# Moving the attention preparation ahead of the threshold search and merging the list's comparisons, in a deformable-convolution and attention kernel

## The chip, the cores and the metric

The kernel runs on one core of a Trainium2 chip. The metric is the device time of one execution in microseconds. Before the change the median of three runs is 10539.41 us (10536.02 to 10541.7). One further execution was profiled; its times are a little longer than those of the bare runs, and every time that is read from a trace belongs to it.

Names: PE is TensorE, DVE is VectorE, ACT is ScalarE, POOL is GpSimd, and SP is the engine from which most DMAs are issued. Line numbers (L1300) are those of the kernel before. In the kernel after, lines from L553 on stand four lower down the file, and those behind the new `yield` five lower.

## The reference

The input x holds four images of 64 x 64 positions (4096 tokens) with 256 channels, in fp32. The first layer is a deformable convolution: from the group-normalised image it computes, for each token, group and tap, an offset and a mask, samples the image bilinearly at the moved places, and projects the sum. The second layer treats each image as a sequence of 4096 tokens. Additive attention comes first and a feed-forward network (FFN) on a selection of the tokens second. Cut to what matters here:

```python
x = x + conv(group_norm(x))                       # bilinear samples at learned offsets
t = tokens(x)
n = layer_norm(t)
beta  = tanh((n @ Wt)[:, :, None] + (n @ Wx)[:, None, :] + bh)   # 4096 x 4096 x 32
a     = softmax(beta @ Wa)
t = t + a @ n
n = layer_norm(t)
w = n @ wr + br                                   # one weight per token
sel = the 2047 tokens with the largest w
y = gelu(n[sel] @ w1 + b1) @ w2 + b2              # 256 -> 1024 -> 256
n[sel] = y * w[sel] where selected, else 0;   t = t + that
```

## The kernel before, in words

**Stages in time.** First the offsets and sampling weights of all four images are computed (until about 815 us). Then image 0 is sampled alone (about 815 to 1480 us). Then, for each image n, there is a stretch *between the loops* (L1408 to L1430) and the attention loop of image n (`attention`, from L860). The FFN of image 3 ends the kernel. The sampling of image n+1 runs beside both the stretch and the attention loop of image n.

**The stretch between the loops.** It has three generators, and each `yield` in them ends one portion of instructions:

- *main*, written m: `feed_forward(n-1)`. It loads all tokens of the attention's result into one large tile `v2` (eight DMAs on SP) and the weights w1, w2, b1, b2 (L1247 to L1251). It computes 32 dot products with wr ("dots", four portions of eight). It searches the 2047th largest weight four bits at a time (`kth_largest`, L1200): in each round DVE counts for 15 candidates how many weights are not below them, PE adds the counts over the partitions (pcn, L1207), and DVE picks the digit. `positions` turns flags into places by a matmul and a running sum. Then POOL writes every token to its place in a DRAM array by 32 indirect DMAs, the *scatter* (L1300). ACT computes the base output rows for all tokens and stores them (L1312). At last the selected tokens are worked through in four chunks of 512. The load of a chunk (L1332, on SP) waits for all 32 scatters. ACT normalises (L1340); PE transposes and DVE copies (xT); POOL adds (L1346); PE multiplies by w1 (ph, L1360), ACT applies gelu, PE multiplies by w2 (py, L1366), DVE scales and adds (L1369), and POOL scatters the rows to the output (L1373).
- *prep*, written o: `attention_prep(n)`. It loads the image's tokens t into `v` (L770, eight DMAs), takes mean and variance of 32 tiles (eight portions of four), and normalises on ACT (L802, 32 activations, one portion). Then come eight *units* of 512 tokens with three portions each: transposes (ptt, L780) and a copy vT, projections (pq, L812), a cut at zero on DVE (mm), selections by matmul (pk, L827, and pf, L833), exponentials on ACT (kf, L828, and qe, L835), a store of qe to DRAM, and a minimum over pk on DVE (least).
- *sampling*, written s: `sample_image(n+1)`. Its first portion is `list_tokens` (L537): tokens whose offsets are too large for the main path are listed by comparing, for each of 32 tiles, a row of slot numbers with the token's slot on DVE (`oh`, L552) and multiplying on PE into `pl` (L553). All further portions are *steps*; there are 440 in an image (`STEPS`). Most are one product of 128 x 1024 on DVE (L697) or one addition (L705). A product needs a weight tile `wb` by an SP DMA (L688, two buffers here). Some steps project the sum (pmo, L721, with its POOL addition) or belong to the far tokens (their gathers, L626, run only beside attention).

A string `turns` deals out the portions: each letter asks its generator for one more. What is left of main and prep is emitted after the string, and what is left of the sampling is dealt out beside the attention loop, one step in every block (256 blocks of 512 queries by 128 keys), and a second step in as many blocks as are needed to bring it to its end.

**Who fixes the order.** The DVE instructions of main and prep go through `pinned` (L259, which therefore is the line of them all), and the products and sums of sampling and all of attention's through `keep`: these stay in program order on their engine. A tile scheduler places the others, DMAs among them, and the buffers of the pools bound how far ahead anything may run. Engines and their DMA queues work in order.

For n = 0 there is no `feed_forward`, and for n = 3 there is nothing to sample, so that the letter s does nothing. The stretches that hold all the change are those of n = 1, 2 and 3; the string of n = 0 and the last FFN, which runs alone, keep their order.

Of the kernel before, what the change touches and what calls it, by code (L numbers as in the profile page):

```python
# [9 lines left out]
F32 = mybir.dt.float32  # L10
I32 = mybir.dt.int32
AF = mybir.ActivationFunctionType
ALU = mybir.AluOpType
# [3 lines left out]
P = 128  # L17
NB, H, W, C = 4, 64, 64, 256
L = H * W
NT = L // P  # L20
# [25 lines left out]
def layers_kernel(ctx: ExitStack, tc: tile.TileContext, a, out: bass.AP):  # L46
    nc = tc.nc
# [19 lines left out]
    def load_const(pool, name, shape, src):  # L67
        t = pool.tile(shape, F32, name=name)
        nc.sync.dma_start(out=t, in_=src)  # L69
        return t  # L70
# [139 lines left out]
    tok = cb.tile([P, NT, 2], F32, name="tok")  # L210
    slotr = cb.tile([P, P], F32, name="slotr")
# [22 lines left out]
    S = SimpleNamespace(bank=True, wants=False, gather=True, left=0, tables=[])  # L234

    def bank_taken():
        S.wants = not S.bank
        return S.wants

    @contextmanager  # L240
    def scope(*pools):

        with ExitStack() as st:
            for name, bufs, psum in pools:
                kw = {"space": PSUM} if psum else {}
                setattr(S, name, st.enter_context(tc.tile_pool(name=name, bufs=bufs, **kw)))
            yield
            for name, _, _ in pools:
                delattr(S, name)
# [267 lines left out]
    def positions(fl, vec):  # L517

        pp = S.ps_m.tile([P, 2, NT], F32, tag="pm", name="pp")
        nc.tensor.matmul(pp[:, 0, :], below, fl, start=True, stop=True)  # L520
        nc.tensor.matmul(pp[:, 1, :], ones, fl, start=True, stop=True)
        before = [S.two.tile([P, NT], F32, tag=f"bf{i}", name=f"bf{i}") for i in range(2)]
        vec.tensor_copy(before[0], pp[:, 1, :])
        for i in range(5):
            w = 1 << i
            vec.tensor_copy(before[1][:, :w], before[0][:, :w])
            vec.tensor_add(before[1][:, w:], before[0][:, w:], before[0][:, : NT - w])
            before.reverse()
        sl = before[1]
        vec.tensor_sub(sl, before[0], pp[:, 1, :])  # L530
        vec.tensor_add(sl, sl, pp[:, 0, :])
        return sl, before[0][:, NT - 1 :]

    def list_tokens(n):

        while bank_taken():
            yield  # L540
        fl = S.two.tile([P, NT], F32, tag="fl", name="fl")
        nc.vector.tensor_scalar(fl, omax[:, n, :], 1.0, None, ALU.is_gt)
        sl, total = positions(fl, nc.vector)
        nc.vector.tensor_copy(large[:, n : n + 1], total)

        nc.vector.tensor_scalar(sl, sl, 1.0, None, ALU.add)
        nc.vector.tensor_mul(sl, sl, fl)
        nc.vector.tensor_scalar(sl, sl, -1.0, None, ALU.add)
        pl = S.ps_m.tile([P, 2], F32, tag="pm", name="pl")
        for i in range(NT):  # L550
            oh = S.sb.tile([P, P], F32, tag="oh", name="oh")
            nc.vector.tensor_scalar(oh, slotr, sl[:, i : i + 1], None, ALU.is_equal)  # L552
            nc.tensor.matmul(pl, oh, tok[:, i, :], start=(i == 0), stop=(i == NT - 1))  # L553
        ls = S.two.tile([P, 2], F32, tag="ls", name="ls")
        nc.vector.tensor_copy(ls, pl)

        uf = S.smp.tile([P, 1], F32, tag="uf", name="uf")
        nc.vector.tensor_mul(uf, ls[:, 1:2], spare)
        nc.vector.tensor_sub(uf, spare, uf)
        nc.vector.tensor_add(uf, uf, ls[:, 0:1])  # L560
        return uf
# [106 lines left out]
    def sample_image(n, depth=1):  # L668
# [3 lines left out]

        S.left = STEPS
        uf = yield from list_tokens(n)
        yield
        exact = []
# [63 lines left out]
    def sample_any(n):  # L740

        num = nc.values_load(large[0:1, n : n + 1], min_val=0, max_val=L)
        with tc.If(num > P), scope(
            ("smp", 2, 0), ("two", 2, 0), ("sb", 2, 0), ("dn", 1, 0), ("ps_t", 1, 1), ("ps_m", 1, 1)
        ):
            cur = S.two.tile([P, 1], F32, tag="cur", name="cur")
            nc.vector.tensor_copy(cur, part)
            with tc.For_i(0, NT, 1):
                exact = []
                for _ in exact_rows(n, cur, exact):  # L750
                    pass
                put_rows(n, *exact[0])
                nc.vector.tensor_scalar(cur, cur, float(P), None, ALU.add)
# [14 lines left out]
    def load_tokens(v, src):  # L768
        for s in range(8):
            nc.sync.dma_start(  # L770
                out=v[:, 4 * s : 4 * s + 4, :C],
                in_=src[s * 512 : (s + 1) * 512].rearrange("(t p) c -> p t c", p=P),
            )
# [470 lines left out]
    def feed_forward(n, vec):  # L1244


        v = S.one.tile([P, NT, C + 4], F32, tag="big", name="v2")  # L1247
        load_tokens(v, t2_d[n])
        w1 = load_const(S.one, "w1", [P, CC, FF], a["L1_ffn_w1"].rearrange("(k p) f -> p k f", p=P))
        w2 = load_const(S.one, "w2", [P, FF // P, C], a["L1_ffn_w2"].rearrange("(k p) f -> p k f", p=P))  # L1250
        b1 = load_columns(S.one, "b1", a["L1_ffn_b1"])  # L1251
# [33 lines left out]
        sl, _ = positions(eq, vec)  # L1285
# [3 lines left out]
        sl, _ = positions(gt, vec)  # L1289
# [65 lines left out]
        for s in range(NSORT // 512):  # L1355
# [7 lines left out]
            for t in range(4):  # L1363
# [8 lines left out]
                m = min(P, NSEL - s * 512 - t * P)  # L1372
# [30 lines left out]
    for n in range(NB):  # L1403
        with scope(("att", 1, 0), ("smp", 2, 0), ("dn", 1, 0)):
            v = S.att.tile([P, NT, C + 1], F32, name="v")
            kf = S.att.tile([P, 2, L], F32, name="kf")

            sampling = sample_image(n + 1) if n + 1 < NB else iter(())  # L1408
            S.gather = False
            with scope(  # L1410
                ("one", 1, 0), ("two", 2, 0), ("sb", 2, 0), ("row", 2, 0), ("rp", 3, 0),
                ("ps_d", 2, 1), ("ps_n", 1, 1), ("ps_m", 3, 1),
            ):


                main = feed_forward(n - 1, pinned) if n else iter(())
                prep = attention_prep(n, v, kf, pinned)
                if n:
                    turns = (
                        "mo" + "m" * 5 + "mo" * 6 + "m" + "ooo" + "s" + "oss" * 2 + "m" + "oss" * 7 + "m" + "oss" * 3  # L1420
                        + ("m" + "ossss" * 3 + "msss" * 4) * 4
                    )
                else:
                    turns = "o" * 10 + "s" + "os" * 24
                for turn in turns:
                    next({"m": main, "o": prep, "s": sampling}[turn], None)
                for rest in (main, prep):
                    for _ in rest:
                        pass
            S.gather = True  # L1430
            with scope(
                ("two", 2, 0), ("sb", 2, 0), ("rp", 6, 0), ("qp", 2, 0),
                ("ep", 2 * PVB + 1, 0), ("ap", 1, 0), ("ps_d", 2, 1), ("ps_n", 3, 1), ("ps_m", 1, 1),
            ):
                attention(n, v, kf, [sampling])
        attention_any(n)
        if n + 1 < NB:
            sample_any(n + 1)
    with scope(("one", 1, 0), ("two", 2, 0), ("sb", 3, 0), ("row", 2, 0), ("ps_d", 2, 1), ("ps_m", 4, 1)):
        for _ in feed_forward(NB - 1, nc.vector):  # L1440
            pass
# [36 lines left out]
```

## Time and profile before

| What | us |
|---|---|
| median of three runs | 10539.41 (10536.02 to 10541.7) |
| profiled execution | 10563.61 |
| its span, first to last instruction | 10561.9 |
| attention loops, first D (L894) to last row sum, n = 0, 1, 2, 3 | 1997, 1912, 1912, 1798 |
| stretch from there to the next first D, before n = 1, 2, 3 | 372, 370, 294 |
| scatter of n = 1 (L1300), first to last | 3680.4 to 3720.7 |
| first ph of n = 1 (L1360) | 3784.5 |
| last FFN alone: end of the scatter, first ph, end of the last py | 10420.8, 10432.8, 10546.3 |

How to read the views. The page counts how long each engine was busy and how many instructions it ran. A *windows* row gives one stretch of time: its borders and length, then for each engine the busy time and in brackets the number of instructions that started, then the mean TensorE clock that was granted (1.00 is full speed), the mean share of the DMA engines in use and GB/s. A *timeline* row gives the start, the time taken, the engine, the line, the operation, output and inputs, the shape, how many alike were joined into the row, and in square brackets how long the engine had been idle before and what ended that ("remote" and "issue" name no instruction). SPq is the DMA queue of SP: its rows last as long as the queue was held. A *group* row gives the busy time and mean duration in nanoseconds of all instructions alike.

### The profile page before, as it was taken

What the parts mean: (1) busy time and instruction counts of PE and PEld (TensorE: products, weight loads), DVE (VectorE), ACT (ScalarE), POOL (GpSimd) and SP (SyncE); (2) the same over time, 40 slices, a digit from 0 to 9 for tenths busy, and PEclk for the clock granted to TensorE, in tenths of its full rate; (3) what the DMA queues carried; (4) which work ended last, traced back from release to release, by engine and by line L of the source; (5) the groups of instructions that cost most, each with busy time, mean ns of one, the idle gap of its engine ahead of it and who ended that gap; (6) DMA issues with size and microseconds to landing.
All of it is one profiled execution on the core that took longest, in us unless ns stands there. A gap on an engine that the chain in (4) does not pass through costs nothing. (4 is left out here: it accounts for less than half of the span.)

```text
span 10561.9 us, 115936 instructions
## 1 busy us (share of the span) xinstructions
PE 9008.4 (85%) x38460; PEld 4375.8 (41%) x38460; DVE 8547.2 (81%) x13406; ACT 7377.6 (70%) x8389; POOL 5265.2 (50%) x3059
## 2 busy tenths in 40 slices
PE   7882029999999678999999589999999699999995
PEld 4551014444444343444444344444444344444443
DVE  7776879898989778989899679899898357777772
ACT  4450018888888528888888438888888379999991
POOL 0004307676555326767655327676555155555552
PEclk8985569999999889999999789999999799999997
DMA  3336752222222252212111352222111300000002
GB/s 119 107 138 180 206 167 70 61 67 64 70 64 73 98 167 60 52 55 58 51 55 50 116 152 53 53 54 54 52 59 41 101 13 9 10 8 7 7 5 75
DMA packets 381330, 766.00 MB, mean 73 GB/s; under 512 B 49105, under 2 KB 212593, under 8 KB 380689
## 3 DMA queue, kind: packets, MB, share of 16 engines
q1 hardware_dynamic: 324432, 678.78, 20.3%
q0 software_dynamic: 30144, 45.87, 2.9%
q10 hardware_dynamic: 26112, 33.56, 0.9%
q8 instruction: 309, 5.06, 0.2%
q14 instruction: 333, 2.72, 0.1%
HBM read 580.88 MB, written 177.14 MB: 72 GB/s over the span
## 5 line engine op out<-in xcount | busy, mean ns | idle before, releaser
L909 DVE TENSOR_TENSOR r<-nn,r 128x512 f32<-128x512 f32 x6144 | 3943.0, 683 | 861.5 <-PE nn L904 805.9
L904 PE MATMUL nn<-qn,kf 32*128 32x512 f32 (+1 forms) x12288 | 4518.8, 640 | 132.7 <-DVE r L909 95.8
L994 POOL TENSOR_TENSOR r<-r 128x1024 f32<-128x1024 f32 x1024 | 2708.8, 2645 | 2645.4 <-DVE r L909 2625.3
L988 ACT ACTIVATE r<-d 128x1024 f32<-128x1024 f32 x3072 | 3117.2, 1015 | 1085.4 <-DVE r L998 699.9
L894 PE MATMUL d<-qf,kf 32*128 32x512 f32 (+1 forms) x12288 | 3338.1, 632 | 76.5 <-DMA qf<-qf 43.1
L990 ACT ACTIVATE r<-r 128x1024 f32<-128x1024 f32 x3072 | 3124.1, 1051 | 32.6
L904 PEld LDWEIGHTS nn<-qn,kf 32*128 32x128 f32 (+1 forms) x12288 | 1399.4, 185 | 1902.1 <-DVE r L909 1450.5
L932 PE MATMUL pv<-v,et 128*128 128x257 f32 x8192 | 2105.3, 400 | 15.0 <-DVE acv L956 15.0
L932 PEld LDWEIGHTS pv<-v,et 128*128 128x128 f32 x8192 | 1507.6, 194 | 975.5 <-issue 768.6
L894 PEld LDWEIGHTS d<-qf,kf 32*128 32x128 f32 (+1 forms) x12288 | 1018.0, 186 | 1340.3 <-issue 736.1
L996 POOL TENSOR_TENSOR r<-r 128x512 f32<-128x512 f32 x1024 | 1335.8, 1304 | 92.7 <-DVE r L909 17.1
L705 DVE TENSOR_TENSOR ac<-ac,prd 128x1024 f32<-128x1024 f32 x768 | 991.8, 1291 | 8.8
L697 DVE TENSOR_TENSOR prd<-xs,wb 128x1024 f32<-128x1024 f32 x768 | 977.7, 1273 | 15.2 <-DMA wb<-wt 12.0
L626 POOL DMA_INDIRECT ga<-tab,tii x576 | 718.3, 1247 | 207.3 <-issue 117.7
L916 ACT ACTIVATE et<-et,nshift 128x512 f32<-128x512 f32 x1024 | 723.8, 707 | 28.2 <-DVE et L1001 28.2
L998 DVE TENSOR_TENSOR r<-r 128x512 f32<-128x512 f32 x1024 | 723.6, 707 | 4.1 <-POOL r L994 3.7
L1001 DVE TENSOR_TENSOR et<-r 128x512 f32<-128x512 f32 x1024 | 698.1, 682 | 0.4
L115 ACT ACT_TABLE_LOAD x9 | 11.5, 1283 | 799.3 <-DVE mv L259 703.0
L721 PE MATMUL pmo<-outwp,ac 128*128 128x256 f32 x512 | 135.7, 416 | 469.1 <-DVE ac L705 431.2
L480 POOL MEMSET w<- 128x1600 f32 x16 | 22.9, 1432 | 675.0 <-PE ptw L497 352.3
L721 PEld LDWEIGHTS pmo<-outwp,ac 128*128 128x128 f32 x512 | 100.8, 205 | 521.4 <-DVE ac L705 304.5
L420 PE MATMUL pc<-xn,diag 128*128 128x512 f32 x576 | 262.2, 609 | 33.4 <-ACT xn L366 33.4
(344 smaller groups left out, 5282.7 us busy)
## 6 DMA issues: line engine op xcount, KB each, us to landing
wb<-wt SPq DMA_DIRECT2D x800, 512.0 KB
tab<-tb SPq DMA_DIRECT2D x128, 256.0 KB
v<-t SPq DMA_DIRECT2D x64, 512.0 KB
xs<-xp SPq DMA_DIRECT2D x32, 680.0 KB
xp<-xp SPq DMA_DIRECT2D x32, 544.0 KB
xt<-in_x_dram SPq DMA_DIRECT2D x32, 512.0 KB
xr<-in_x_dram SPq DMA_DIRECT2D x64, 256.0 KB
t<-xr SPq DMA_DIRECT2D x64, 256.0 KB
```

Source lines behind the costliest of these rows:

```text
L697: keep(nc.vector.tensor_tensor(pr.rearrange("p (r w) -> p r w", w=W), src, wb.rearrange("p (r w) -> p r w", w=W), ALU.mult,))
L705: keep(nc.vector.tensor_add(ac[:, f, :], ac[:, f, :], pr))
L894: keep(nc.tensor.matmul(d[:, j, :], kf[g, blk, rows(kt)], qs[q][0][g, blk, :], start=True, stop=True))
L904: keep(nc.tensor.matmul(nn, kf[g, blk, rows(kt)], qs[q][1][g, blk, :], start=True, stop=True))
L909: keep(nc.vector.tensor_tensor(r[:, j, :], ns[j], r[:, j, :], ALU.mult))
L916: keep(nc.scalar.activation(ets[b], ets[b], AF.Exp, bias=nshift))
L932: keep(nc.tensor.matmul(pv, ets[b0 + i][:, rows(j)], v[:, k0 + i, :], start=(i == 0), stop=(i == PVB - 1)))
L988: keep(nc.scalar.activation(rs[b, p], ds.pop((b, p)), AF.Ln))
L990: keep(nc.scalar.activation(rs[b, p], rs[b, p], AF.Exp, scale=-1.0))
L994: keep(nc.gpsimd.tensor_tensor(rs[b, 1], rs[b, 1], rs[b, 2], ALU.add))
L996: keep(nc.gpsimd.tensor_tensor(rs[b, 1][:, 0], rs[b, 1][:, 0], rs[b, 3][:, 0], ALU.add))
L998: keep(nc.vector.tensor_add(rs[b, 1][:, 1], rs[b, 1][:, 1], rs[b, 3][:, 1]))
```

## The change

It has three parts.

1. In `list_tokens` the slots of two tiles are compared by one `tensor_tensor` on 128 x 2 x 128 elements with both inputs broadcast, in place of two `tensor_scalar` on 128 x 128. The 32 matmuls stay as they are.
2. A `yield` behind the load of v2 splits the first portion of main in two.
3. The string `turns` for n of 1 and more is another.

```diff
         for i in range(NT):
-            oh = S.sb.tile([P, P], F32, tag="oh", name="oh")
-            nc.vector.tensor_scalar(oh, slotr, sl[:, i : i + 1], None, ALU.is_equal)
-            nc.tensor.matmul(pl, oh, tok[:, i, :], start=(i == 0), stop=(i == NT - 1))
+            if i % 2 == 0:
+                oh = S.sb.tile([P, 2, P], F32, tag="oh", name="oh")
+                nc.vector.tensor_tensor(
+                    oh, slotr.rearrange("p (o q) -> p o q", o=1).to_broadcast([P, 2, P]),
+                    sl[:, i : i + 2].rearrange("p (t o) -> p t o", o=1).to_broadcast([P, 2, P]), ALU.is_equal,
+                )
+            nc.tensor.matmul(pl, oh[:, i % 2], tok[:, i, :], start=(i == 0), stop=(i == NT - 1))
...
         load_tokens(v, t2_d[n])
+        yield
         w1 = load_const(S.one, "w1", [P, CC, FF], a["L1_ffn_w1"].rearrange("(k p) f -> p k f", p=P))
...
                     turns = (
-                        "mo" + "m" * 5 + "mo" * 6 + "m" + "ooo" + "s" + "oss" * 2 + "m" + "oss" * 7 + "m" + "oss" * 3
-                        + ("m" + "ossss" * 3 + "msss" * 4) * 4
+                        "om" + "o" * 9 + "s" + "om" * 12 + "m" + "oss" * 4 + "m" + "oss" * 8 + "m"
+                        + ("m" + "s" * 8 + "msss" * 4) * 4
                     )
```

Read letter by letter, the strings deal out this:

| | before | after |
|---|---|---|
| first loads | v2 with w1, w2, b1, b2, then v | v, then v2 |
| w1, w2, b1, b2 | with v2 | with the first dots |
| statistics of v (8 portions) | 6 beside the search, 2 behind the scatter's letter | all ahead of the dots |
| normalising | behind the scatter's letter | ahead of the dots |
| the list | behind the scatter's letter | ahead of the dots |
| portions of units beside dots and search | none | 12 of 24 |
| from the scatter's letter to that of the first chunk | 9 portions of units, 18 steps | 12 portions, 24 steps |
| from there to the first ph | 3 portions, 6 steps | none |
| in the FFN's four chunks | 12 portions, 96 steps | 80 steps |
| steps left for the attention loop | 320 | 336 |

## The prediction

> **What bounds the kernel now.** I read the page first, then the busy time by stretches, then the timelines of single engines inside the stretches that the change touches. The page:
>
> ```profile
> span 10561.9 us, 115936 instructions
> PE 9008.4 (85%) x38460; PEld 4375.8 (41%) x38460; DVE 8547.2 (81%) x13406; ACT 7377.6 (70%) x8389; POOL 5265.2 (50%) x3059
> ```
>
> No engine is full over the whole; the stages have different limits, and the change touches only the stretch between two attention loops. By the first D (L894) and the last row sum of each image these stretches are 3607 to 3979 (372 us), 5910 to 6280 (370) and 8211 to 8505 (294). Stretches by engine (stretch, length, then busy us and instructions of each engine, granted clock of PE, DMA share, GB/s):
>
> ```profile
> 3607.00:3680.00 73.00, 8.79 (x32) 7.65 (x32) 52.06 (x261) 19.09 (x34) 0.15 (x1) 0.51 0.71 237
> 3680.00:3735.00 55.00, 22.45 (x83) 18.41 (x84) 14.94 (x65) 17.44 (x34) 31.83 (x33) 0.50 0.22 78
> 3735.00:3785.00 50.00, 42.04 (x83) 15.91 (x83) 46.59 (x59) 11.57 (x16) 3.24 (x1) 0.69 0.58 172
> 3785.00:3850.00 65.00, 62.35 (x199) 35.84 (x198) 47.43 (x46) 26.48 (x32) 7.32 (x5) 0.97 0.52 167
> 3850.00:3955.00 105.00, 89.01 (x311) 58.23 (x309) 91.49 (x89) 25.93 (x31) 24.84 (x16) 0.95 0.62 199
> 3955.00:3980.00 25.00, 1.79 (x10) 0.63 (x10) 9.20 (x13) 0.00 (x0) 6.76 (x4) 0.54 0.46 134
> 3980.00:5910.00 1930.00, 1869.22 (x8293) 862.16 (x8286) 1733.09 (x2611) 1645.89 (x1792) 1232.12 (x685) 0.98 0.19 52
> ```
>
> Search and scatter (first two rows): PE idle at half clock; during the scatter (3680 to 3721) DVE is idle for 40 of 55 us. Then DVE and PE together bound the FFN, with sampling and the second half of the preparation on DVE. In all DVE is busy 261.7 of 373 us, idle 111. In attention DVE is busy 90%.
>
> Why is the scatter empty? The timelines of POOL, DVE, ACT and SP (start, us, operation, count, and in brackets the idle time before it with its releaser):
>
> ```profile
> 3683.02 0.96 POOL L1300 DMA_INDIRECT sort<-v,rif  x1 [0.30 <-issue]
> ```
>
> ```profile
> 3707.23 0.29 DVE L552 TENSOR_SCALAR oh<-slotr,bf 128x128 f32<-128x128 f32 x1 [5.34 <-remote]
> 3731.59 1.22 DVE L259 COPY vT<-ptt 128x1024 f32<-128x1024 f32 x1
> ```
>
> ```profile
> 3687.04 15.84 ACT L802 ACTIVATE v<-v,lnm,lnr 128x256 f32<-128x256 f32 x32 [1.79 <-DMA sort<-v,rif]
> 3702.90 1.28 ACT L828 ACT_TABLE_LOAD   x1
> ```
>
> ```profile
> 3649.04 92.32 SPq L688 DMA_DIRECT2D wb<-wt  x4
> 3741.67 0.92 SPq L1332 DMA_DIRECT2D big<-sort  x2
> ```
>
> The 32 scatters take 1.27 us each (40.3 us). Beside them stand only the list's comparisons, which crawl on late PE results, and the normalising. The first unit of the preparation starts at 3731. The sorted rows' load stands on SP behind the wb loads, 21 us past the last scatter (3720.7).
>
> **The change part by part.** For n=1:
>
> (1) *Everything of the preparation up to the normalising, and the list, come ahead of the search.* Today the first count (pcn, L1207) is at 3632.4 and the threshold at 3670.1: 37.7 us, of which 5 x 4 row statistics (2.12 us per four in the timeline) are 10.6, so the bare search is 27.1. Afterwards DVE starts at about 3617.7, when the first tokens land, as now. Eight groups of statistics (17 us) interleave with the list: 16.1 us where it runs alone (819.7 to 835.6), mostly waiting for its 32 matmuls, with under 10 us of DVE. Together some 28 us, to 3646. The 32 activations (15.84) and the table load (1.28) come next; the first exponential is behind them on ACT, the reduction least is pinned on DVE behind that, and the dots are pinned behind least. So this wait, hidden in the scatter today, is bare: +17.1, to about 3667 with PE's part. Dots (13.5) and the next unit's copies: first count near 3682, 50 us later than now.
>
> (2) *Four units of the preparation beside the search.* A unit is 8 transposes, 4 pq, 4 pk and pf: at half clock 2.1 + 3.8 + 3.8 = 9.7 us of PE (4 pq took 3.78 at 3732.9). Its copy, mm and least cost DVE 1.22 + 0.74 + 1.22 = 3.2; about two units' worth lies inside the search, 6.6. A count stands in PE's queue behind a unit's matmuls and the next candidate behind the count; bounds for this wait: 0 (count first) to 29 us (three units, fully serial). I take 6. Search 27.1 + 6.6 + 6 = 40, against 37.7. Scatter starts near 3731, **+51 us**.
>
> (3) *Four units and 16 sampling steps beside the scatter.* Steps alternate a product (L697, 1.22 us) and an add (L705): 16 x 1.23 = 20 us of DVE, and 4 x 3.2 = 13 for units. They pay only because DVE was idle here. POOL's gathers show the price of such company:
>
> ```profile
> 964.78 1.97 POOL L626 DMA_INDIRECT ga<-tab,tii  x1 [0.30 <-issue]
> 967.05 0.96 POOL L626 DMA_INDIRECT ga<-tab,tii  x1 [0.30 <-issue]
> ```
>
> Beside a full stream of products three take 4.79 us, 1.60 each. The scatter is thus between 40.5 and 51 us; DVE is half filled, so 45: end at 3776. The Trainium skill ("SBUF — State Buffer", section "Who interferes with whom") speaks both against and for this: a vector instruction with two SBUF inputs locks out GpSimd's reads, yet it infers that descriptor writing is untouched; by that inference the scatter would stay at 40.5, by the row up to 51. The row decides.
>
> (4) *The sorted load.* In the new SP order eight wb loads, then both sorted loads, which wait for the last scatter; wb loads behind them wait too. So DVE runs out at the ninth product and the idle 40 us come back in part. In the last FFN, without company, ph follows the last scatter's end by 12 us (10420.8 to 10432.8); today by 64. I take 25, between: ph at 3801 against 3784.5, **+16.5**.
>
> (5) *FFN without preparation and with 80 steps for 96.* DVE from the first FFN copies to the last (3774.8 to 3961) is 186.2: 123.5 products and adds, 12.9 units, 32.8 idle, of which 11.66 one wait for a unit's transposes. Remove 16 steps (20), the units (12.9) and that wait with its small fellows (12.8): 140. PE alone needs 113.7 (last FFN) + 6.9 for sampling's pmo = 120.6, so DVE still bounds. Last update at 3941 instead of 3960.5. The tail to the first D stays at 18.7 (a q load from DRAM, written long before). **Gain per stage: 19.5, say 20**; 39 if PE bounds, 8 if the search takes 46 and the scatter 51.
>
> (6) *Steps pushed into attention.* 440 steps per image are fixed; 104 instead of 120 run here, so attention(1) and (2) take 336 instead of 320. Attention(0) with 415 steps left to it (25 are dealt before) took 1997.4 us (1592.4 to 3589.8), attention(1) with 320 1912.4 (3978.8 to 5891.2): 85 us for 95 steps, 0.89 each; a block with two steps takes 8.27 against 6.9 with one: 1.3. Sixteen cost 14.3 to 20.8; I take 17.5. **-35 for two images.** Most of the gain of (5) is only moved.
>
> (7) *n=3*, no sampling: here the path is serial.
>
> ```profile
> 8284.00:8330.00 46.00, 16.82 (x42) 8.16 (x42) 10.36 (x23) 19.72 (x37) 30.68 (x32) 0.61 0.32 108
> 8330.00:8505.00 175.00, 157.88 (x536) 93.53 (x536) 39.20 (x65) 58.18 (x73) 26.52 (x20) 0.95 0.14 48
> ```
>
> Scatter today 8283.8 to 8324.1, ph 8349.4, last py 8489.2. All that stands ahead of the search now (17 statistics less 10.6, 17.1 ACT, 13 units, waits; no list) moves the scatter by +40, to 8324; end 8365, ph at about 8379, and an FFN free of units takes 113.7 to 118: 8493 to 8497. **4 to 8 us later, say 6** (bounds: 15 earlier if normalising is covered, 15 later if the search is 46).
>
> (8) *List comparisons.* 32 of 292 ns (L552) become 16 of two blocks. No 128x256 comparison is in the trace; nearest are 128x128 at 0.29 and L909's 128x512 at 0.68: 0.42 between them, bounds 0.29 and 0.68. So 9.3 becomes 6.7 us of DVE, but the list waits for PE's 32 matmuls (46 waits for pl in L552's row). I take 0; bounds -3 and +6 for each of four lists.
>
> Sum: -2 x 20 + 35 + 6 + 0 = **+1 us**. The profiled execution took 10563.61 us (span 10561.9); the median of the runs is 10539.41, 0.23% below it. I put the difference on the median: **10540 us, no change**. A measurement tells about 0.2% (21 us) from nothing.
>
> **The rivals.** *Even trade* (forecast): idle time moves from the scatter to the front and to the sorted load, and steps only change their place. Its own range, with a gain of 8 to 32 per stage and n=3 by 15 either way: 10515 to 10565; chance 0.42 (faster 0.06, same 0.30, slower 0.06).
>
> *Faster, PE-bound FFN*: the scatter is filled, units do not meet counts, the FFN falls to 121 instead of 140: 39 per stage, -78 + 35 + 6 = -37: 10502; with the sorted load at 12 us after the scatter, 13 more in two stages: 10476. For it: DVE's 111 us of idle; against: the SP order and the bare normalising. 0.32.
>
> *Slower, the search behind the units on PE*: nine counts per search queue behind cold unit matmuls. Fully serial 27.1 + 29 + 6.6 = 63 instead of 40, +23 in three stages: 10609; half of it: 10575. It makes the kernel slower by more than 0.2% once a search takes over 47 us. For it: PEclk 0.51 in the first row and in-order queues; against: from 3735 to 3785, with PE busy 42 of 50 us, the clock rose to 0.69, and PE's own part of a count is 0.6 us. 0.20. The Trainium skill ("TensorE: Matmul & The Clock Gate", "Part 1: The HAM clock gate") says that some 3.4 us of steady work open the clock in full; as an estimate by that page, three units beside the search would take half of their cold time and this rival would lose about half of its price.
>
> *It does not do what it says*: beside the scatter PE's results reach DVE 5 us late, as in the 3707 row; four units with three handoffs each need 60 us, so preparation ends only after the scatter and holds the FFN: +15 per stage, 10585. 0.06.
>
> **How the numbers follow.** Faster 0.06 + 0.32 = 0.38; same 0.30; slower 0.06 + 0.20 + 0.06 = 0.32. The range reaches into both sides: 10485 to 10592.
>
> **What would show it.** First count at 3682 and scatter at 3731 right means (1) and (2); DVE idle under 20 us beside the scatter means (3); SP holding both sorted loads with a wb load late behind means (4); last update 20 us earlier means (5); attention(1) and (2) longer by 15 to 21 means (6); n=3's first D at 8505 plus 6, on its stage's own clock, means (7). A scatter that starts as early as now, or a stage shorter by over 40, makes the prediction wrong.

## The result, and the profile after

Over 13 runs each the kernel after takes 10556.04 us (median; 10537.18 to 10566.75) and the kernel before 10536.02 us (10523.73 to 10542.81). The ratio is 1.0020, with a 95% interval from 1.0012 to 1.0028: slower by 0.2%, at the edge of what the prediction called no change. The forecast was 10540 and the range 10485 to 10592.

One thing has to be known first. The execution of the kernel before that was profiled at first took 10563.61 us, 28 us more than the median of its bare runs, and the one of the kernel after took 10553.13 us, 3 us less than its own. By these two profiles alone the change would be a gain of 10 us. A second trace of each was therefore taken. In the table a *stretch* runs from the last row sum of one attention loop to the first D of the next (the table of the part on the kernel before starts it some 18 us later, at the last sum of the values), and a *loop* from the first D to the last row sum.

| us | before, 1st trace | before, 2nd | after, 1st | after, 2nd |
|---|---|---|---|---|
| stretch n=1 | 388.9 | 369.5 | 380.0 | 376.2 |
| stretch n=2 | 388.7 | 373.2 | 373.1 | 373.5 |
| stretch n=3 | 313.6 | 314.7 | 313.0 | 312.6 |
| loop n=1 | 1912.5 | 1911.7 | 1920.1 | 1918.8 |
| loop n=2 | 1911.9 | 1909.9 | 1920.8 | 1920.7 |
| span | 10561.9 | 10520.3 | 10551.4 | 10549.9 |

Between the second traces the stretches cost +6.7, +0.3 and -2.1 and the two loops +7.1 and +10.8: +23 us, which is the size of the measured difference. The loop of n=0 and the part ahead of it, in which the change touches only the list's comparisons, differ by up to 10 us each from trace to trace, so that a single trace tells nothing below that of the whole; a stretch is read more finely (below).

The page after, and its stretches (columns as before: stretch, length, busy us and instructions of PE, PEld, DVE, ACT, POOL, granted clock, DMA share, GB/s). The second fence is of n=1: up to the first count, the search, the scatter, up to the first ph, the FFN.

```profile
span 10551.4 us, 115967 instructions
PE 9060.6 (86%) x38460; PEld 4413.7 (42%) x38460; DVE 8528.1 (81%) x13342; ACT 7330.7 (69%) x8356; POOL 5286.5 (50%) x3059
```

```profile
3590.00:3686.00 96.00, 57.93 (x190) 39.57 (x191) 53.13 (x235) 23.74 (x42) 1.15 (x2) 0.65 0.46 148
3686.00:3737.00 51.00, 33.10 (x76) 16.93 (x74) 29.86 (x115) 22.19 (x37) 0.17 (x1) 0.57 0.33 114
3737.00:3784.00 47.00, 26.86 (x48) 10.28 (x48) 25.45 (x23) 4.10 (x4) 37.55 (x32) 0.61 0.52 177
3784.00:3810.00 26.00, 7.27 (x24) 4.52 (x24) 17.92 (x14) 8.38 (x12) 6.35 (x3) 0.57 0.63 208
3810.00:3950.00 140.00, 126.16 (x425) 81.47 (x426) 109.94 (x113) 26.74 (x41) 25.62 (x19) 0.95 0.55 178
```

The same for the second trace of the kernel before: up to the scatter, the scatter, up to the first ph, the FFN.

```profile
3589.00:3680.00 91.00, 24.06 (x98) 19.74 (x98) 56.42 (x275) 19.43 (x35) 0.77 (x2) 0.60 0.58 195
3680.00:3721.00 41.00, 28.05 (x104) 20.55 (x103) 18.27 (x64) 19.50 (x36) 31.24 (x33) 0.62 0.36 130
3721.00:3768.00 47.00, 28.36 (x62) 11.16 (x63) 42.09 (x55) 9.72 (x14) 3.36 (x2) 0.68 0.49 159
3768.00:3935.00 167.00, 151.44 (x508) 94.13 (x506) 137.48 (x134) 52.33 (x63) 32.38 (x21) 0.96 0.57 188
```

The FFN, from the first ph to the end of the last py, is 27 us shorter (167 to 140); that it would become shorter was foreseen. But what stands ahead of it is longer by about 40: 220 us to the first ph in this trace of after (217 in the other), 179 before. DVE has hardly more to do beside the scatter than before (25 us of 47, against 18 of 41), and it stands still for some 8 of the 26 us behind it.

Where DVE waits in the stretch of n=1 (what waits and for what: us in total, times, longest), before (second trace) and after (second trace), four groups of each; the waits of 13.2 us for the loop's last sums are the same in both and left out:

```profile
DVE pos L594 <- DMA rw<-raw,rii: 16.6, 1, 16.6
DVE vT L259 <- PE ptt L780: 11.7, 1, 11.7
DVE prd L697 <- DMA wb<-wt: 6.9, 8, 2.0
DVE kflag L259 <- PE pcn L1207: 5.6, 8, 0.7
```

```profile
DVE prd L701 <- DMA wb<-wt: 31.5, 12, 25.1
DVE xr L732 <- POOL xr L729: 18.6, 4, 7.3
DVE kflag L259 <- PE pcn L1211: 15.6, 8, 2.8
DVE least L259 <- ACT kf L832: 6.4, 1, 6.4
```

The waits for the far tokens' gather and for a unit's transposes are down to 3.6 and 1.8 us. In their place come longer ones for weights, behind the sorted load (31.5 against 6.9), for POOL's addition in the projections (18.6 against 4.5) and for the counts, behind unit matmuls (15.6 against 5.6), and one for the first exponential (6.4). These four are 72 us; the four shown of before are 41.

### The profile page after: what moved, and what is told of

It reads as the page before. It is cut to its first block, busy times and chain, and to the rows that moved or that the text cites. A ratio compares the mean times of both kernels' runs of the same rounds, so it can differ in the third digit from the quotient of the medians.

```text
span 10551.4 us, 115967 instructions
## 1 busy us (share of the span) xinstructions
PE 9060.6 (86%) x38460; PEld 4413.7 (42%) x38460; DVE 8528.1 (81%) x13342; ACT 7330.7 (69%) x8356; POOL 5286.5 (50%) x3059
## 3 DMA queue, kind: packets, MB, share of 16 engines
q1 hardware_dynamic: 324432, 678.78, 19.7%
## 5 line engine op out<-in xcount | busy, mean ns | idle before, releaser
L1000 POOL TENSOR_TENSOR r<-r 128x512 f32<-128x512 f32 x1024 | 1330.1, 1299 | 90.8 <-DVE r L913 15.8
L1305 POOL DMA_INDIRECT sort<-v,rif x128 | 137.5, 1074 | 400.6 <-DVE rif L259 284.3
```

What stands on the lines that cost most here:

```text
L1000: keep(nc.gpsimd.tensor_tensor(rs[b, 1][:, 0], rs[b, 1][:, 0], rs[b, 3][:, 0], ALU.add))
```

## The experiments

Times are medians of their own runs; ratios are against the kernel before on the same chip, with 95% intervals. Stretches and loops are from one trace of each kernel. Stretches that should be alike differ by up to 4 us between traces, loops by up to 12 (steps_back has the same steps in both of its loops).

| kernel | us | ratio | stretches n=1, 2, 3 | loops n=1, 2 |
|---|---|---|---|---|
| again_before | 10527.4 | 0.9998 (0.9989 to 1.0007) | 369.5, 373.2, 314.7 | 1911.7, 1909.9 |
| again_after | 10555.8 | 1.0024 (1.0015 to 1.0033) | 376.2, 373.5, 312.6 | 1918.8, 1920.7 |
| list_only | 10529.3 | 1.0002 (0.9993 to 1.0011) | 372.1, 376.1, 314.6 | 1909.2, 1910.9 |
| order_only | 10538.4 | 1.0007 (0.9997 to 1.0016) | 371.1, 367.6, 313.1 | 1923.4, 1922.7 |
| late_pos | 10548.4 | 1.0014 (1.0005 to 1.0023) | 364.5, 371.2, 312.9 | 1926.7, 1929.8 |
| steps_back | 10577.5 | 1.0042 (1.0029 to 1.0056) | 391.2, 387.6, 313.0 | 1911.1, 1922.7 |
| dots_first | 10518.5 | 0.9986 (0.9977 to 0.9995) | 358.2, 361.9, 307.0 | 1929.8, 1918.5 |
| pool_load | 10541.9 | 1.0009 (1.0000 to 1.0018) | 371.9, 368.1, 315.7 | 1923.2, 1918.7 |
| fewer_steps | 10531.1 | 1.0004 (0.9995 to 1.0013) | 359.2, 357.4, 317.9 | 1922.2, 1923.0 |
| units_late | 10553.7 | 1.0023 (1.0014 to 1.0032) | 374.5, 371.9, 313.1 | 1923.9, 1922.1 |
| both | 10520.7 | 0.9988 (0.9979 to 0.9997) | 363.2, 361.5, 315.7 | 1921.3, 1921.7 |
| both_64 | 10525.7 | 0.9996 (0.9987 to 1.0005) | 344.8, 352.5, 309.2 | 1943.0, 1944.4 |

### The two kernels once more

> The kernel before, unchanged, for a second trace of it. Its first profiled execution (10563.6 us) lies 27 us above the median of its bare runs (10536.0), that of the kernel after (10553.1) 3 us below its own (10556.0). Theory 1 (that execution was slow somewhere outside the changed stretches, by the clock or by the DMAs): a second one comes out near 10540, and the stretch that is shorter can be read off; the stretches between the loops stay at 372, 370 and 294 us. Theory 2 (the stretches themselves vary): they differ by over 5 us between the two traces.

> The kernel after, unchanged. The runs known of it lie at 10537 to 10541 and at 10552 to 10567. Even-trade theory: the two stretches shorter by 9 to 16 us, the loops of n=1 and 2 longer by 8 to 18, n=3 unchanged, as in its first trace, ratio 1.001 to 1.003. Rival (the difference sits outside the changed stretches and is the clock's): a trace in which stretches and loops agree with the first within 3 us, and the time differs by 15.

The second trace of before is 42 us shorter than the first, and 35 us of that lie in the two stretches, not outside: Theory 2 held. In the first trace the list beside the scatter took 50 us, with PE's results reaching DVE late ("remote", shown in the prediction). In the second it took 18, and the first unit's copy vT stands at 3698 instead of 3731. The waits of DVE in n=1 of the first trace, and its timeline in the second, which has no such wait in any stretch:

```profile
DVE oh L552 <- remote: 30.8, 7, 7.4
```

```profile
3691.75 0.29 DVE L552 TENSOR_SCALAR oh<-slotr,bf 128x128 f32<-128x128 f32 x1 [0.25 <-PE pl L553]
3697.82 0.16 DVE L555 COPY ls<-pl 128x2 f32<-128x2 f32 x1 [1.21 <-PE pl L553]
3698.48 1.22 DVE L259 COPY vT<-ptt 128x1024 f32<-128x1024 f32 x1
```

So the empty scatter that the prediction meant to fill was mostly a trait of that one execution: none of the 13 other traces here has a wait of DVE that ends with "remote", and in the traces of list_only and fewer_steps, which order the work ahead of the first ph as before, ph comes 179 to 182 us into the stretches of n=1 and 2, as in the second trace, and not at 195. What delayed PE's results in the first stays open. The two traces of after agree within 4 us in every stretch and loop of the table.

### The two halves of the change

list_only is the kernel before with the first block of the diff; order_only is the kernel after without it.

> The kernel before with the list's comparisons of two tiles in one instruction, and nothing else. Even-trade theory: 0 (-3 to +6 us for each of four lists), the list of image 0 alone still about 16 us, held by 32 matmuls. Rival (the new instruction's two inputs in SBUF block the scatters beside it): scatter longer than 41 us and the list ends later than 10 us after it, up to +6 us for each of three.

> The kernel after with the list's single-tile comparisons of before: new order alone. Even-trade theory: the time of the kernel after within 5 us, since the list ahead of the search is interleaved with statistics and waits for PE. If merging pays in this place: up to 16 x 0.16 = 2.6 us of DVE for each of two lists, 5 us slower than the kernel after.

In the old order merging is worth nothing, as expected: the list, from its first comparison to its last matmul, shrinks from 18.4 to 14.6 us in the stretch, and nothing follows from it. In the new order neither expectation held. order_only is 17 us *faster* than the kernel after (the intervals only just touch), though its list takes longer, 18.9 us against 14.3. ACT's timeline tells where: the normalising waits for the last row statistic, which is later in the kernel with the merged list. First order_only, then after; each first row is the same operation of the FFN's part, at the start of the stretch.

```profile
3616.63 0.32 ACT L115 ACTIVATE lnr<-tmv,eps 128x32 f32<-128x32 f32 x1
3641.43 0.32 ACT L115 ACTIVATE lnr<-mv,eps 128x32 f32<-128x32 f32 x1 [24.47 <-DVE mv L259]
```

```profile
3616.41 0.32 ACT L115 ACTIVATE lnr<-tmv,eps 128x32 f32<-128x32 f32 x1
3649.37 0.32 ACT L115 ACTIVATE lnr<-mv,eps 128x32 f32<-128x32 f32 x1 [32.64 <-DVE mv L259]
```

25 us from one to the other without merging, 33 with it; 24 and 32 at n=2. (At n=3, where there is no list, it is 22 in both.) On DVE's queue the scheduler puts one operation of another chain between every two row statistics. With 32 comparisons these gaps are all taken by the list. With 16 the list is through with some 13 statistics still to come, and the next operations of the far tokens move into the gaps, among them two that read a gathered row (pos), which has not landed: DVE stands 3.5 us there with the last statistics behind it.

late_pos keeps just these two in program order:

```diff
-            nc.vector.scalar_tensor_tensor(
+            keep(nc.vector.scalar_tensor_tensor(
                 pos[:, o], rw[:, o * GP : (o + 1) * GP], hw[:, o : o + 1], txy[:, o], ALU.add, ALU.add
-            )
+            ))
```

> The kernel after, with the two operations that read the gathered row rw (pos, L598) kept in program order, so that the scheduler can't hoist them among the last row statistics. Theory (merging halves the list's instructions, the list ends ten statistics early, and DVE then waits 3.5 us in pos for the gather and does the far tokens' arithmetic before the normalising may start): statistics end some 7 us earlier, near 3642 instead of 3649, the scatter of n=1 and 2 starts 5 to 7 us earlier, the time is 10 to 17 us under the kernel after, that is within 10 of the kernel before. Rival (order_only is faster for another reason, its list keeps PE busy until the units): the scatter does not move by over 2 us.

The statistics end 4 us earlier (29 us behind the same mark; 28 at n=2), not 7; the rest of the delay is the far tokens' other small operations, which are still between the statistics. The scatter starts 10 us earlier than in again_after at n=1, but only 1.7 at n=2, where by its own measure the rival holds. The time falls by 7 us, less than was expected, and the intervals overlap. That the hoisted operations delay the normalising is shown by the traces; that they account for all 17 us is not.

### The steps that moved into the loops

steps_back is the kernel after with `"s" * 12` for `"s" * 8`. fewer_steps is the kernel before with `"oss" + "osss" * 2` for `"ossss" * 3`. Each moves 16 steps per image and nothing else.

> The kernel after, with four more sampling steps in each of the FFN's four chunks: 96 steps there as before, 320 left for the attention loop. Even-trade theory: loops of n=1 and 2 back by 7 to 11 us each to 1911, the FFN longer by 16 x 1.25 = 20, ratio 1.003 to 1.005. Rival (PE bounds the FFN, DVE has room): the stretch stays within 5 us, the kernel is 10 to 20 us faster than the kernel after.

> The kernel before, with four sampling steps fewer in each of the FFN's four chunks (80 instead of 96) and nothing else, so that the attention loops take 336 steps. Theory from the runs so far (a step costs 0.6 to 0.8 us in the loop and about 0.8 in the stretch): stretches of n=1 and 2 12 to 20 us shorter, loops 7 to 12 longer, 5 to 20 us faster than the kernel before in total, so that the new order alone is worth less than nothing. Rival (an even trade): within 5 us of the kernel before.

In fewer_steps the stretches shrink by 10.3 and 15.8 us and the loops grow by 10.5 and 13.1, and the time stays: the trade is even, as the prediction said, at about 0.8 us a step in the stretch and 0.7 in the loop. In steps_back the stretches grow by 15 and 14, and the loops give back 8 at n=1 and nothing at n=2; the time is some 20 us over that of the kernel after, so that there the trade is not even. One loop alone is a poor measure: over all traces above but that of both_64, the 18 loops with 336 steps average 1922.6 us and the eight with 320 1912.5, which is 0.6 us a step.

The FFN's length goes with its steps in both kernels, so they stand on its path. That DVE alone bounds it is not shown: in the FFN of the kernel after PE is busy for 126 of 140 us and DVE for 110. Of the 27 us by which it is shorter after the change, some 8 (6.8 and 9.5 in fewer_steps, from the first ph to the last py) are steps that moved, and are paid in the loops; what is left goes with the units that left it.

### What holds the FFN back

units_late deals no unit ahead of the scatter:

```diff
-                        "om" + "o" * 9 + "s" + "om" * 12 + "m" + "oss" * 4 + "m" + "oss" * 8 + "m"
+                        "om" + "o" * 9 + "s" + "m" * 13 + "oooss" * 4 + "m" + "oooss" * 4 + "s" * 8 + "m"
```

> The kernel after, with all units of the preparation behind the scatter's letter: none beside dots and search. It tells what the units cost the search. Theory (counts queue behind cold unit matmuls, some 2 us in each of nine, and the first units' wait for the normalising stands ahead of the dots): scatter of n=1 starts 25 to 40 us earlier, but eight units need 50 to 80 us of PE behind it and hold the first ph, which moves by less than 12; n=3 within 10. Rival (the time to the scatter sets the stretch): ph as much earlier as the scatter, 60 us or more faster in total.

The scatter starts 45 and 39 us earlier than in again_after (at 100 us instead of 145 in n=1), and the first ph moves by 2.4 and 1.5 us only. In n=3 as well: ph at 184 us against 182. The search without units takes 25.8 us, against 41.1 in the kernel after. So the time to the scatter alone does not set the stretch. From the scatter's end to the first ph it is now 73 us, where it was 26, with eight units to do there instead of four, and not by their own work only. Waits of ACT and of DVE in n=1, from the scatter's start to the first ph:

```profile
ACT big L1345 <- DMA big<-sort: 26.4, 1, 26.4
DVE least L259 <- ACT kf L832: 31.3, 4, 24.6
```

ACT has taken up the normalising of the first chunk (L1345) and holds its queue until the sorted rows land, some 6 us behind the scatter; a unit's exponential kf stands behind it, and least on DVE and all further units behind that. So some 25 us of the time that was won ahead of the scatter are lost to this wait.

pool_load takes the sorted loads off SP's queue:

```diff
-            get = nc.sync.dma_start(
+            get = nc.gpsimd.dma_start(
                 out=xs, in_=sort_d[n][s * 512 : (s + 1) * 512].rearrange("(t p) c -> p t c", p=P)
```

> The kernel after, with the loads of the sorted chunks issued from POOL's queue, behind the scatters, instead of SP's. Theory (SP stands at the first sorted load from 3755 to 3786 and the wb loads behind it starve DVE for 26 us): that idle time goes, ten or so products and sums move into the scatter's window, the FFN has as many fewer, 10 to 20 us faster than the kernel after in total. Rival (DVE's sums there slow the scatter, and its end sets the stretch): the scatter grows by up to 4 us and the time stays.

In the kernel after DVE and ACT both stand still beside the scatter's second half and past its end (3784). Timeline of DVE, then of ACT:

```profile
3791.43 1.22 DVE L701 TENSOR_TENSOR prd<-xs,wb 128x1024 f32<-128x1024 f32 x1 [26.08 <-DMA wb<-wt]
```

```profile
3789.38 2.07 ACT L1345 ACTIVATE big<-big 128x256 f32<-128x256 f32 x4 [26.47 <-DMA big<-sort]
3791.36 1.00 ACT L839 ACTIVATE qe<-pf 128x1024 f32<-128x1024 f32 x1
```

DVE waits for weights whose load is behind the sorted load on SP; ACT waits for the sorted rows themselves, with an exponential of a unit in its queue behind that. In pool_load the first wait goes and the second takes its place (DVE's waits in n=1):

```profile
DVE least L259 <- ACT kf L832: 29.3, 2, 22.7
DVE prd L701 <- DMA wb<-wt: 7.0, 11, 1.2
```

The stretches are 4 and 5 us shorter and that of n=3 3 us longer. The time is 14 us under the kernel after, with intervals that overlap: by the size the theory was right; by the trace the two stretches gain 10 us and the two loops lose 2, so that only half of it can be seen.

### The bare normalising

dots_first deals the dots ahead of the first unit, so that DVE has them while ACT normalises:

```diff
-                        "om" + "o" * 9 + "s" + "om" * 12 + "m" + "oss" * 4 + "m" + "oss" * 8 + "m"
+                        "om" + "o" * 9 + "s" + "m" * 4 + "om" * 8 + "m" + "ooss" * 4 + "m" + "oss" * 8 + "m"
```

> The kernel after, with the dots dealt ahead of the first unit, which covers the normalising (15.84 us) and the table load on ACT; four portions of units go from the search to the scatter's window. Theory (that wait on DVE is bare in the kernel after): first count 10 to 14 us earlier in all three stretches, scatter as much or more earlier; 25 to 40 us faster than the kernel after if the time up to the scatter sets the end of the stretch. Rival (the work beside the scatter decides, and four more portions there use up the gain): scatter earlier, first ph the same within 4 us.

The first counts come 26, 24 and 17 us earlier than in again_after (10 to 14 were expected), the scatters start 23, 19 and 17 us earlier, ph comes 18, 13 and 4 earlier, and the stretches are 18, 12 and 6 us shorter. The time is 37 us under the kernel after and 0.14% under the kernel before: with both, below, the only order of these whose interval lies under 1. In n=1 DVE uses the first count's result at 3655, before the first exponential (3660); in the kernel after it did so at 3687, 19 us behind it (3668). Four portions of units moved behind the scatter's letter along with it; how much of the gain is theirs the runs do not tell. The timeline of ACT:

```profile
3642.56 15.84 ACT L806 ACTIVATE v<-v,lnm,lnr 128x256 f32<-128x256 f32 x32 [1.20 <-DVE lnm L259]
3659.71 1.02 ACT L832 ACTIVATE kf<-pk 128x1024 f32<-128x1024 f32 x1
```

The last two put the parts together; both_64 has `"s" * 4` for `"s" * 8` besides.

> dots_first and pool_load together: the dots ahead of the units and the sorted loads from POOL's queue. If the two waits are independent: 10 to 14 us under dots_first, near 10505. If the scatter's end sets the stretch in dots_first already: the same as dots_first within 5 us.

> As both, with 64 sampling steps in the FFN instead of 80 (352 left for the loops). If DVE still bounds the FFN: stretches of n=1 and 2 10 to 18 us shorter than in both, loops 6 to 12 longer, 5 to 15 us faster in total. If PE bounds it (at about 121 us of FFN): stretches at most 8 shorter, and 0 to 15 us slower.

both equals dots_first: the loads on POOL add nothing, since the wait on ACT is left (28.3 us of waits for kf in its stretch of n=1, the longest 19.7). In both_64 the stretches of n=1 and 2 shrink by 18 and 9 us and the loops grow by 22 and 23: a step in the loop now costs 1.4 us, twice the price of the 16 before it. Its time is 5 us over that of both, with intervals that overlap, so 64 steps in the FFN are no better than 80. In all these strings the first chunk's letter stands behind the last portion of the units already; it is the scheduler that puts ACT's part of the chunk ahead of their last exponentials. To keep these in program order on ACT, which should clear its queue, was not tried.

## Why the prediction was right, and where its steps were not

The number was right within its range, and no change was nearly so: 10556 against 10540. But it is near in part by luck, since errors in opposite directions went into the sum. Foreseen were -40 for two stretches, +35 for two loops, +6 for n=3 and 0 for the list, in all +1. Between the second traces they are +7, +18 and -2, in all +23: 47 us missed in the stretches, of which 25 were made up elsewhere.

*The base, (5).* "Gain per stage: 19.5" was reckoned against the first trace's stretch, in which ph came at 195 us. In the second trace it comes at 179. The prediction's times for the kernel *after* are near: first count 3682 (measured 3686.4), the search 40 us (41 in n=1, 37.5 in n=2 and 3), the scatter 3731 to 3776 (3736.8 to 3784.0), ph 3801 (3810), the FFN, which it reckoned from DVE's first copy to its last update, 140 (145). Against the first trace the stretches gain 9 to 16 us. What failed is the subtraction: against the second trace of before those of n=1 and 2 lose 7 and 0 us instead of gaining 20. The view to distrust was at hand: the profiled execution was 0.23% above the median, and the prediction put that on the median as a constant, though 35 of the 42 us sat in the very windows under study. The 20 us taken for 16 steps were too many as well: in fewer_steps DVE's time from first copy to last update falls by 10 and 13.

*The steps, (6).* 17.5 us a loop was foreseen and 7 to 13 measured (0.4 to 0.8 us a step), 10 by the average of all traces. The price was taken between 0.9 and 1.3; only the next 16 steps cost that, or a little more (1.4, both_64).

*The list, (8).* "I take 0; bounds -3 and +6": in the old order 0 is right. In the new order it holds up the normalising by some 8 us in each of two stretches, not through the instruction (0.42 us, as taken) but through where the scheduler then puts its neighbours.

*Right:* (1) the bare normalising, in that the first count comes 19 us behind the first exponential, and 4 ahead of it in dots_first, with 37 us of gain; but DVE has the first dots and the units' copies to do meanwhile, so that its wait for that exponential is 6.5 us and not 17.1; (2) counts behind unit matmuls (15.6 us of waits against 5.6 in n=1, where 6 more were taken); (3) a scatter of 46 to 49 us against 40.7, near the 45 taken, though DVE is idle for 21.5 us beside it, just over the 20 that were set as the sign; (4) SP held by the sorted load, with DVE out of work for 26 us. In (4) ACT was overlooked: its queue is held by the same load, in units_late too. (7): scatter +38 for +40 and ph +24 for +30, but the end 2 us earlier instead of 6 later: 6 of these 8 are ph's, and the rest is the FFN of n=3, which takes 114 us, the lower end (140 before).

Of the rivals, the slower one had the right sign and the wrong price: the search is 41 us, under its 47, and yet the kernel is at the 0.2% line. The faster one, with an FFN of 121 us bounded by PE, did not come: it takes 140, and 124 only with 16 more steps taken out of it (both_64). Late PE results beside the scatter, the fourth, did not come in either trace of after.

## What to carry to other kernels

Work that moves ahead of a serial chain lengthens the chain; it pays only if the idle window it fills is there in other executions too, so compare a profiled execution's time with the bare median, and take a second trace before building on a wait that names no instruction. Look in each in-order queue at what stands behind an instruction that waits, on all queues at once: with a late transfer at the head of both SP and ACT, clearing SP alone left DVE to wait 22.7 us for ACT, and an earlier scatter (units_late) left it 24.6. And fewer instructions are no gain in themselves where a scheduler fills gaps one by one: what moves up into the free gaps may wait.

## What the runs showed of the hardware

The scatter of 32 indirect DMAs takes 40.2 to 40.7 us with little beside it and 46.1 and 48.7 us beside products and sums on DVE (again_after, n=1 and 2), 44 in dots_first. The Trainium skill ("SBUF — State Buffer", section "Who interferes with whom") infers that two-input vector operations leave descriptor writing alone; here the scatters beside them are slower by 13 to 20%, and the traces show which operation goes with it. Two scatters of the kernel after on POOL, and what DVE does meanwhile, a minimum over pk and then a sum:

```profile
3750.97 0.96 POOL L1305 DMA_INDIRECT sort<-v,rif  x1 [0.30 <-issue]
3752.24 1.95 POOL L1305 DMA_INDIRECT sort<-v,rif  x1 [0.30 <-issue]
3751.01 1.22 DVE L259 TENSOR_REDUCE least<-pk 128x1 f32<-128x1024 f32 x1
3752.14 1.22 DVE L709 TENSOR_TENSOR ac<-ac,prd 128x1024 f32<-128x1024 f32 x1
```

Of the 32 scatters at n=1 of this trace, the 17 with no product or sum beside them take 0.96 us each, and the 15 with one take 1.43 on average, up to 1.99; that is 7 us in all, the whole difference between this scatter (47.2 us) and one of 40.2. At n=3, where there are copies and minima on DVE but no products, all 32 stay at 0.96 on average in both kernels.

PE's clock stayed low beside the search although PE was busy for 33 of 51 us (0.57 in the row from 3686), and rose to 0.95 in the FFN with 126 of 140. The rule of "TensorE: Matmul & The Clock Gate" ("Part 1: The HAM clock gate"), by which a few microseconds of steady work open the clock, agrees as far as the work in the search is not steady: around the counts PE stops for up to 1.9 us at a time.

That DVE can stand for up to 14 us with no instruction of the program to name for it was not expected: such waits cost 30.8 us in n=1 of the first trace of before (14.0 in one of n=3), while both traces of after and the second of before have none over 3 us, and no other trace here has one that ends with "remote".
